# Two attention layers: score tiles in two PSUM pairs, one bank per accumulator, and other split steps in the second layer

## The chip, the cores and the metric

The kernel runs on one core of a Trainium2 chip. The metric is device time in microseconds (us), lower is better. Three runs of the kernel before took 3214.86, 3215.67 and 3217.78 us; their median is 3215.67. The engines are called PE (matmul), PEld (the weight loads ahead of matmuls, which overlap them), DVE (vector), ACT (scalar, activations), POOL and SP (which here mostly issue DMAs).

## The reference

The input x is (4, 64, 64, 256): four images of 4096 tokens with 256 channels, in float32. Two self-attention layers follow each other.

```
# layer 0, per image; x is 4096 x 256
q, k = x @ Wq + bq, x @ Wk + bk          # 4096 x 32
v = x @ Wv + bv                          # 4096 x 256
x = gamma * (softmax(q @ k.T) @ v) + x
# layer 1
f, g = x @ Wf + bf, x @ Wg + bg          # 4096 x 32 (keys, queries)
v = x @ Wh + bh                          # 4096 x 128
out = x + (softmax(g @ f.T) @ v) @ Wo + bo
```

## The kernel before

Both layers are done as flash attention without a running maximum: scores are computed transposed (keys on partitions), their exponential is the unnormalised weight p, p is multiplied with the values into PSUM, and the division by the sum comes at the end of a block of queries.

**Two kinds of product.** An fp32 matmul takes two records on PE for each instruction. An fp32r matmul takes one[...]. So a step can be *split*: ACT computes the exponential twice (`high`, L537, with a slightly lowered exponent and rounded to fp32r, and `p`, L539, in fp32), and DVE makes `low = p - high` (L543) and `d = high - 4096 low` (L548). Three fp32r products with three forms of the values (h, l, d) then give the fp32 product: h and l go to one accumulator, d to another, and at the block's end they are combined as `(1 + EPS) * first + second`. A step that is not split is called whole: it has one exponential and one fp32 product, which goes straight into the second accumulator.

**Layer 0** has 16 blocks of 256 queries per image, with 8 steps of 512 keys each. All steps are split. A step has four score matmuls of 256 columns (L527) and 24 products of 258 columns (L567): 256 channels, one column for the sum of the weights and one of padding. There are two halves of 128 queries, each with its two accumulators, so four accumulators in all. The block's end (`end_first`, L600, L601) copies the first accumulator of a half on ACT and adds the second on DVE; divisions, the residual and the output follow as small units in the next block's steps.

**Layer 1** has 8 blocks of 512 queries per image, with 16 steps of 256 keys each. A step has two score matmuls of 512 columns, and products with two 128-key tiles (L585). The steps in `SPLIT1` (2, 6, 10, 14) are split, the other twelve are whole. The sum of the weights is added up on DVE over the steps (L560; L558 adds the first two). The block's end (`end_second`) has two ACT copies of halves of the first accumulator (L637), two DVE adds of the second (L638) and a DVE add of the sum's two halves (L640). Then four output units, in steps 1 to 4 of the next block, each multiply 128 queries with Wo and compute their sum of weights on PE (L647, L648), and divide and store them.

**The order of work.** The main loop (L719 on) runs over all steps of both layers and all images. In step n it issues `cut_both` of n (d), `cut_low` of n+1, the sum's add of n, the scores and the exponentials of n+2, units that are due in this step, and the products of n. In layer 1 the d products of a split step come after the products of the step behind it. The units project the next stretch of tokens: layer 1's queries, keys and values while layer 0 runs (the last two in the first block of layer 1), and the next image's layer 0 while layer 1 runs (none in the last image). A unit transposes tokens (L389), splits them (L402, L403), multiplies them (L419, L461) and brings queries and keys through DRAM to their places (SP stores, POOL loads, L490). This is the order in which the kernel is written; the framework's scheduler may still move instructions of an engine past each other when it builds the program, and it adds the waits. Each engine runs its instructions in the built order.

**PSUM** has eight banks of 512 fp32 values per partition. `ps_st` holds one score tile of two banks, for both layers: the scores of step n+2 can be written when the exponentials of step n+1 have read it. `ps_acc` has four banks in rotation: layer 0 takes all four for a block, layer 1 takes two, so that one block's accumulators lie beside the next one's. `ps_side` has two banks for units. In SBUF the buffers that matter are tags "p" (three, whole p), "t" (two, `high`, and p of layer 1's split steps), "l" (two) and "d" (one: d of layer 0, the running sum of layer 1).

Of the kernel before, what the change touches and what calls it, by code (L numbers as in the profile page):

```python
# [49 lines left out]
F32 = mybir.dt.float32  # L50
F32R = mybir.dt.float32r
I32 = mybir.dt.int32
AF = mybir.ActivationFunctionType
# [3 lines left out]
P = 128  # L57
QB = 512
QB0 = 256
# [3 lines left out]
EPS = 2.0**-12  # L63
UP = 2.0**12
AHEAD = 3

SPLIT1 = (2, 6, 10, 14)

# [166 lines left out]
def fast_path(ctx: ExitStack, tc: tile.TileContext, x, w0, w1, wo, bo, gamma, out, off):  # L237

    nc = tc.nc
# [5 lines left out]
    W = C + 2  # L245
    assert C == 2 * P and CV == (C, P) and D == 32 and N % QB == 0
    G = (4, 2)
    NQ = (N // QB0, N // QB)
    NI = (N // (G[0] * P), N // (G[1] * P))
    NS = QB0 // P  # L250
# [5 lines left out]
    data = ctx.enter_context(tc.tile_pool(name="data", bufs=1))  # L256
    work = ctx.enter_context(tc.tile_pool(name="work", bufs=2))
    dram = ctx.enter_context(tc.tile_pool(name="dram", bufs=1, space=bass.MemoryType.DRAM))
    ps_st = ctx.enter_context(tc.tile_pool(name="ps_st", bufs=1, space=bass.MemoryType.PSUM))
    ps_acc = ctx.enter_context(tc.tile_pool(name="ps_acc", bufs=4, space=bass.MemoryType.PSUM))  # L260
    ps_side = ctx.enter_context(tc.tile_pool(name="ps_side", bufs=2, space=bass.MemoryType.PSUM))


# [106 lines left out]

    xT, x_parts, k_t, v_t, halves = {}, {}, {}, {}, {}
    qk_dram, x1_dram = {}, {}
    q_t, first_p, waiting = {}, [], {}


    def transpose_unit(b, l, h):
# [134 lines left out]
    class Step:  # L511
# [8 lines left out]
        def scores(self):  # L520
            b, l, j, i = self.b, self.l, self.j, self.i
            n = 2 * QB // G[l]
            q0 = j * n % QB
            st = ps_st.tile([P, G[l], n], F32, tag="st", name=f"st_{self.key}")
            for g in range(G[l]):
                kt = G[l] * i + g
                nc.tensor.matmul(  # L527
                    st[:, g, :],
                    k_t[b, l, kt // NT][:, kt % NT * P : (kt % NT + 1) * P],
                    q_t[b, l, j * n // QB][:, q0 : q0 + n],  # L530
                    start=True,
                    stop=True,
                )
            s_flat = st.rearrange("p g n -> p (g n)")
            if self.split:
                self.high = wide("t", f"high_{self.key}", F32R)
                nc.scalar.activation(self.high, s_flat, AF.Exp, bias=down)  # L537
            self.p = wide("t" if self.split and l == 1 else "p", f"p_{self.key}")
            nc.scalar.activation(self.p, s_flat, AF.Exp)  # L539
# [12 lines left out]
        def add_up(self, p_sum):  # L552
            if self.l == 0:
                return
            if self.i == 0:
                first_p.append(self.p)
            elif self.i == 1:
                nc.vector.tensor_add(p_sum, first_p.pop(0), self.p)  # L558
            else:
                nc.vector.tensor_add(p_sum, p_sum, self.p)  # L560

# [13 lines left out]
        def products_second(self, acc, parts):  # L575
            v = v_t[self.b, self.i]
            for part in parts:
                p, v_part, which, first, last = {
                    "h": lambda: (self.high, v["h"], 0, self.i == SPLIT1[0], False),
                    "l": lambda: (self.low, v["l"], 0, False, self.i == SPLIT1[-1]),  # L580
                    "d": lambda: (self.d, v["d"], 1, False, False),
                    "whole": lambda: (self.p, v, 1, self.first, self.last),
                }[part]()
                for g in range(G[1]):
                    nc.tensor.matmul(  # L585
                        acc[which],
                        v_part[:, g, :],
                        p[:, g * QB : (g + 1) * QB],
                        start=first and g == 0,
                        stop=last and g == G[1] - 1,  # L590
                    )
# [36 lines left out]

        return [residual(0), residual(1)]

    def end_second(b, j, acc, p_sum):
        key = f"{b}_{j}"
        o = []
        for h in range(QB // QB0):
            part = slice(h * QB0, (h + 1) * QB0)
            o.append(work.tile([P, W], F32, tag="o", name=f"o_{key}_{h}"))
            nc.scalar.activation(o[h][:, :QB0], acc[0][:, part], AF.Copy, scale=1.0 + EPS)  # L637
            nc.vector.tensor_add(o[h][:, :QB0], o[h][:, :QB0], acc[1][:, part])  # L638
        sums = work.tile([P, QB], F32, tag="sums", bufs=1, name=f"sums_{key}")
        nc.vector.tensor_add(sums, p_sum[:, :QB], p_sum[:, QB:])  # L640

        def output(t):
            def issue():
                tok = slice(t * P, (t + 1) * P)
                ps = side_psum(f"pso_{key}_{t}")
                part = o[t // NS][:, t % NS * P : (t % NS + 1) * P]
                nc.tensor.matmul(ps[:, :C], part, wo_sb, start=True, stop=True)  # L647
                nc.tensor.matmul(ps[:, C : C + 1], sums[:, tok], ones[:, :1], start=True, stop=True)  # L648
                n = (b * N + j * QB) // P + t
                nc.vector.reciprocal(inverse[:, 1, n : n + 1], ps[:, C : C + 1])  # L650

                y = small(f"y_{key}_{t}")
                nc.scalar.activation(y, ps[:, :C], AF.Copy, scale=inverse[:, 1, n : n + 1])  # L653
                row = j * QB + t * P
                nc.gpsimd.dma_start(out[b, row : row + P, :], y, accum_op=ALU.add)  # L655

            return issue

        return [output(t) for t in range(NT)]
# [15 lines left out]
    steps[1].scores()  # L675
    steps[0].cut_low()
    beyond = Step(B, 1, 0, 0)
    beyond.scores = nothing
    keys = [(b, l, j) for b in range(B) for l in range(2) for j in range(NB)][NB:]
    acc, p_sum, units = None, None, {}  # L680

# [33 lines left out]
    for n, s in enumerate(steps):  # L715
        b, l, j = s.b, s.l, s.j
        if s.first:
            units = plan(b, l, j, ends)
            acc = [  # L719
                ps_acc.tile([P, QB], F32, tag="acc", name=f"acc_{b}_{l}_{j}_{a}") for a in range(2 * NS if l == 0 else 2)  # L720
            ]
            if l == 1:
                p_sum = wide("d", f"p_sum_{b}_{j}")
        if l == 0 and s.last:
            x_res[b, j] = []
            for t in range(NS):
                x_res[b, j].append(small(f"x_res_{b}_{j}_{t}"))
                row = (j * NS + t) * P
                nc.sync.dma_start(x_res[b, j][t], x[b, row : row + P, :])
                nc.gpsimd.tensor_add(x_res[b, j][t], x_res[b, j][t], bv)  # L730

        ahead = steps[n + 3] if n + 3 < len(steps) else None
        if ahead is not None and ahead.first:
            k = (ahead.b, ahead.l, ahead.j * (QB0, QB)[ahead.l] // QB)
            if k not in q_t:
                load_q(*k)
        if b == l == j == 0 and s.i == 5:
            load_q(0, 0, 0, slice(QB0, QB), qk_dram[0, 0, 0].bitcast(F32R)[:, :, :, QB0:])
        after, later = (steps[n + k] if n + k < len(steps) else beyond for k in (1, 2))

        early = []
        if b == l == j == 0 and s.i + AHEAD < NB:
            early = [project_units(0, 0, 2 * (s.i + AHEAD) + k) for k in range(2)]
            run([u[0] for u in early])

        s.cut_both()
        after.cut_low()
        s.add_up(p_sum)
        todo = units.get(s.i, [])

        if l == 1:
            later.scores()
            run(todo)

            behind = steps[n - 1] if not s.first and steps[n - 1].split else None
            if s.last and behind:
                behind.products_second(acc, ("d",))
            s.products_second(acc, ("h", "l") if s.split else ("whole",))
            if not s.last and behind:
                behind.products_second(acc, ("d",))  # L760
        else:
            for half, what in ((0, "h"), (0, "l"), (1, "h")) if s.last else ((0, "h"), (1, "h")):
                s.products_first(acc, half, what)
            for half in () if s.last else (0, 1):
                s.products_first(acc, half, "l")
            if early:
                run(early[0][1:] + early[1][1:])
            later.scores()
            run(todo)
            for half, what in ((0, "d"), (1, "l"), (1, "d")) if s.last else ((0, "d"), (1, "d")):  # L770
                s.products_first(acc, half, what)

        over = (min(s.i + 2, NI[l] - 1) + 1) * G[l] // NT if j == NQ[l] - 1 else 0
        while keys and halves.get(keys[0]) == 2 and (keys[0][:2] == (b, l) or keys[0][2] < over):
            load_k(*keys.pop(0))
        if s.last:
            ends = end_first(b, j, acc) if l == 0 else end_second(b, j, acc, p_sum)
    run(ends)


# [67 lines left out]
```

## Time and profile before

| what | value |
|---|---|
| median of three runs | 3215.67 us |
| the profiled execution, and its span | 3218.27 us, 3216.5 us |
| granted PE clock | 0.997 |
| layer 0 stages, images 2 to 4 (elapsed) | 454.2, 453.5, 452.7 us |
| layer 1 stages, images 1 to 4 (elapsed) | 336.2, 336.3, 336.0, 312.6 us |
| DVE busy in the layer 1 stage of image 2 | 287.5 us |
| exponential p, 128x1024 (L539) | 1020 ns each |
| exponential high, 128x1024 (L537) | 1116 ns each |
| DVE add of the sum, 128x1024 (L560) | 1222 ns each |

The times are of one profiled execution. "Busy" is the time in which an engine had an instruction under way. A matmul's end is modelled, and matmuls overlap in the pipeline, so the mean duration of one is longer than the distance between two. "Idle before" is the time that an engine stood still ahead of an instruction, and the name after the arrow is what ended it. "Issue" there means that nothing visible was waited for.

### The profile page before, as it was taken

What the parts mean: (1) busy time and instruction counts of PE and PEld (TensorE: products, weight loads), DVE (VectorE), ACT (ScalarE), POOL (GpSimd) and SP (SyncE); (2) the same over time, 40 slices, a digit from 0 to 9 for tenths busy, and PEclk for the clock granted to TensorE, in tenths of its full rate; (3) what the DMA queues carried; (4) which work ended last, traced back from release to release, by engine and by line L of the source; (5) the groups of instructions that cost most, each with busy time, mean ns of one, the idle gap of its engine ahead of it and who ended that gap; (6) DMA issues with size and microseconds to landing.
All of it is one profiled execution on the core that took longest, in us unless ns stands there. A gap on an engine that the chain in (4) does not pass through costs nothing. (4 is left out here: it accounts for less than half of the span.)

```text
span 3216.5 us, 53556 instructions
## 1 busy us (share of the span) xinstructions
PE 3166.9 (98%) x19780; PEld 2637.3 (82%) x19780; DVE 2688.0 (84%) x3221; ACT 2081.7 (65%) x2771; POOL 758.6 (24%) x948
## 2 busy tenths in 40 slices
PE   8999999999999999999999999999999999999997
PEld 7999997666799999766679999966668999995554
DVE  7888888888888888888888888888888888887776
ACT  6666666666666666666666666666666666666564
POOL 5222223111322222211132222311123222241110
PEclk9999999999999999999999999999999999999999
DMA  4121113222311112322231121222222112131111
GB/s 117 43 50 49 46 49 73 38 40 42 60 45 50 49 44 54 67 40 41 41 63 41 47 52 46 66 52 40 44 48 51 46 46 52 43 74 27 24 22 16
DMA packets 368348, 155.56 MB, mean 48 GB/s; under 512 B 264112, under 2 KB 352688, under 8 KB 368080
## 3 DMA queue, kind: packets, MB, share of 16 engines
q1 hardware_dynamic: 322048, 100.76, 12.9%
q0 software_dynamic: 45120, 50.97, 9.5%
q8 instruction: 160, 2.62, 0.4%
q14 instruction: 108, 0.88, 0.1%
q10 hardware_dynamic: 912, 0.33, 0.0%
HBM read 82.58 MB, written 67.11 MB: 47 GB/s over the span
## 5 line engine op out<-in xcount | busy, mean ns | idle before, releaser
L539 ACT ACTIVATE p<-st 128x1024 f32<-128x1024 f32 x1024 | 1044.7, 1020 | 283.9 <-PE st L527 276.7
L537 ACT ACTIVATE high<-st,down 128x1024 fp32r<-128x1024 f32 x640 | 714.3, 1116 | 710.1 <-PE st L527 572.5
L543 DVE TENSOR_TENSOR low<-p,high 128x1024 fp32r<-128x1024 f32 x640 | 859.6, 1343 | 159.2 <-ACT p L539 159.2
L548 DVE SCALAR_TENSOR_TENSOR d<-low,high 128x1024 fp32r<-128x1024 f32 x640 | 788.6, 1232 | 227.7 <-PE acc L567 225.0
L527 PE MATMUL st<-q,k 128*128 128x256 f32 (+1 forms) x3072 | 744.8, 350 | 6.7 <-ACT p L539 5.4
L585 PE MATMUL acc<-p,v 128*128 128x512 f32 x1536 | 735.6, 596 | 0.0
L527 PEld LDWEIGHTS st<-q,k 128*128 128x128 f32 x3072 | 455.9, 189 | 192.2 <-ACT p L539 130.7
L567 PE MATMUL acc<-v0d,d 128*128 128x258 f32 x4096 | 593.1, 284 | 2.6 <-DVE d L548 2.2
L567 PE MATMUL acc<-v0h,high 128*128 128x258 f32 x4096 | 588.5, 283 | 1.2 <-ACT high L537 1.2
L567 PE MATMUL acc<-v0l,low 128*128 128x258 f32 x4096 | 588.3, 283 | 0.6 <-DVE low L543 0.5
L560 DVE TENSOR_TENSOR p_sum<-p_sum,p 128x1024 f32<-128x1024 f32 x448 | 547.3, 1222 | 14.2 <-ACT p L539 3.6
L567 PEld LDWEIGHTS acc<-v0h,high 128*128 128x128 f32 x4096 | 534.5, 190 | 1.6 <-ACT high L537 1.4
L567 PEld LDWEIGHTS acc<-v0d,d 128*128 128x128 f32 x4096 | 530.5, 189 | 5.2 <-DVE d L548 4.5
L567 PEld LDWEIGHTS acc<-v0l,low 128*128 128x128 f32 x4096 | 532.3, 189 | 1.1 <-DVE low L543 1.0
L585 PEld LDWEIGHTS acc<-p,v 128*128 128x128 f32 x1536 | 282.5, 189 | 186.5 <-issue 158.8
L624 POOL TENSOR_TENSOR x_res<-x,bo 128x256 f32<-128x256 f32 x128 | 200.8, 1569 | 891.2 <-DVE x L613 891.1
L490 POOL DMA_DIRECT2D q<-qk_dram x256 | 127.4, 509 | 706.0 <-PE st L527 701.4
L655 POOL DMA_DIRECT2D out<-y x128 | 113.0, 891 | 507.6 <-ACT y L653 502.3
L461 PE MATMUL psv<-wv,xT 128*128 128x128 f32 (+1 forms) x1024 | 196.6, 332 | 2.7 <-DVE v0d L479 1.4
L730 POOL TENSOR_TENSOR x_res<-x_res,bv 128x256 f32<-128x256 f32 x128 | 171.0, 1336 | 72.7 <-DMA x_res<-in_x 72.5
L461 PEld LDWEIGHTS psv<-wv,xT 128*128 128x128 f32 x1024 | 160.0, 193 | 20.4 <-DVE v0d L479 2.2
L490 POOL DMA_DIRECT2D k<-qk_dram x224 | 113.4, 524 | 221.0 <-PE st L527 109.2
(97 smaller groups left out, 2069.5 us busy)
## 6 DMA issues: line engine op xcount, KB each, us to landing
x_res<-in_x SPq DMA_DIRECT2D x128, 128.0 KB, 2.1
qk_dram<-qk_parts SPq DMA_DIRECT2D x128, 128.0 KB, 1.8
x_dram<-x SPq DMA_DIRECT2D x128, 128.0 KB, 1.7
out<-x_res SPq DMA_DIRECT2D x128, 128.0 KB, 1.7
squares<-x_dram SPq DMA_DIRECT2D x512, 32.0 KB, 2.0
out<-y POOLq DMA_DIRECT2D x128, 128.0 KB, 3.1
q<-qk_dram POOLq DMA_DIRECT2D x252, 64.0 KB, 2.2
k<-qk_dram POOLq DMA_DIRECT2D x224, 64.0 KB, 2.1
```

Source lines behind the costliest of these rows:

```text
L461: nc.tensor.matmul(ps[:, t, :], xT[key][:, c, t * P : (t + 1) * P], wv[l][:, c, :], start=(c == 0), stop=(c == NCC - 1),)
L490: nc.gpsimd.dma_start(dst[n * D : (n + 1) * D, :], parts[h, which])
L527: nc.tensor.matmul(st[:, g, :], k_t[b, l, kt // NT][:, kt % NT * P : (kt % NT + 1) * P], q_t[b, l, j * n // QB][:, q0 : q0 + n], start=Tru ...
L537: nc.scalar.activation(self.high, s_flat, AF.Exp, bias=down)
L539: nc.scalar.activation(self.p, s_flat, AF.Exp)
L543: nc.vector.tensor_sub(self.low, self.p, self.high.bitcast(F32))
L548: nc.vector.scalar_tensor_tensor(self.d, self.low.bitcast(F32), -UP, self.high.bitcast(F32), ALU.mult, ALU.add)
L560: nc.vector.tensor_add(p_sum, p_sum, self.p)
L567: nc.tensor.matmul(acc[2 * s + which][:, :W], p[:, g * QB0 + s * P : g * QB0 + (s + 1) * P], v0[self.i][v][:, g, :], start=self.first and ...
L585: nc.tensor.matmul(acc[which], v_part[:, g, :], p[:, g * QB : (g + 1) * QB], start=first and g == 0, stop=last and g == G[1] - 1,)
L624: nc.gpsimd.tensor_add(x_old[s], x_new[s], bo_sb)
L730: nc.gpsimd.tensor_add(x_res[b, j][t], x_res[b, j][t], bv)
```

## The change

The score tiles and accumulators of both layers move into one pool, `ps_main`, with named places: "st" (two banks), "pair" (two banks), "acc0" and "acc1" (one bank each). In layer 1 the scores of a step go to "pair" if the step's number within the image is even and not 0, and to "st" otherwise, so two score tiles alternate. Its two accumulators are acc0 and acc1 in every block. In layer 0 the scores stay in "st", and the third and fourth accumulators are the two halves of one "pair" tile.

The split steps become 0, 4, 8 and 12. So the first step of a block is split and writes the first accumulator alone, and the last is whole and writes the second one alone; the second one's first product is now that of step 1. The running sum starts as a copy of p of step 0, and every later step adds. The ACT copies of the first accumulator become a function of their own, `take_first_two`, which is called in the last step ahead of the scores of n+2. In layer 0, the first step of a block takes the order of products that only the last had: first half h and l, second half h, and then, after the scores and units, d, l, d.

```diff
-SPLIT1 = (2, 6, 10, 14)
+SPLIT1 = (0, 4, 8, 12)
...
-    ps_st = ctx.enter_context(tc.tile_pool(name="ps_st", bufs=1, space=bass.MemoryType.PSUM))
-    ps_acc = ctx.enter_context(tc.tile_pool(name="ps_acc", bufs=4, space=bass.MemoryType.PSUM))
+    ps_main = ctx.enter_context(tc.tile_pool(name="ps_main", bufs=1, space=bass.MemoryType.PSUM))
     ps_side = ctx.enter_context(tc.tile_pool(name="ps_side", bufs=2, space=bass.MemoryType.PSUM))
...
-            st = ps_st.tile([P, G[l], n], F32, tag="st", name=f"st_{self.key}")
+            index = j * NI[1] + i
+            tag = "pair" if l == 1 and index > 0 and index % 2 == 0 else "st"
+            st = ps_main.tile([P, G[l], n], F32, tag=tag, name=f"st_{self.key}")
...
             if self.i == 0:
-                first_p.append(self.p)
-            elif self.i == 1:
-                nc.vector.tensor_add(p_sum, first_p.pop(0), self.p)
+                nc.vector.tensor_copy(p_sum, self.p)
             else:
                 nc.vector.tensor_add(p_sum, p_sum, self.p)
...
-                    "whole": lambda: (self.p, v, 1, self.first, self.last),
+                    "whole": lambda: (self.p, v, 1, self.i == 1, self.last),
...
-    def end_second(b, j, acc, p_sum):
-        key = f"{b}_{j}"
+    def take_first_two(b, j, acc):
+
         o = []
         for h in range(QB // QB0):
-            part = slice(h * QB0, (h + 1) * QB0)
-            o.append(work.tile([P, W], F32, tag="o", name=f"o_{key}_{h}"))
-            nc.scalar.activation(o[h][:, :QB0], acc[0][:, part], AF.Copy, scale=1.0 + EPS)
-            nc.vector.tensor_add(o[h][:, :QB0], o[h][:, :QB0], acc[1][:, part])
+            o.append(work.tile([P, W], F32, tag="o", name=f"o_{b}_{j}_{h}"))
+            nc.scalar.activation(o[h][:, :QB0], acc[0][:, h * QB0 : (h + 1) * QB0], AF.Copy, scale=1.0 + EPS)
+        return o
+
+    def end_second(b, j, acc, p_sum, o):
+        key = f"{b}_{j}"
+        for h in range(QB // QB0):
+            nc.vector.tensor_add(o[h][:, :QB0], o[h][:, :QB0], acc[1][:, h * QB0 : (h + 1) * QB0])
...
-            acc = [
-                ps_acc.tile([P, QB], F32, tag="acc", name=f"acc_{b}_{l}_{j}_{a}") for a in range(2 * NS if l == 0 else 2)
-            ]
+            acc = [ps_main.tile([P, QB], F32, tag=f"acc{a}", name=f"acc{a}_{b}_{l}_{j}") for a in range(2)]
+            if l == 0:
+                pair = ps_main.tile([P, 2, QB], F32, tag="pair", name=f"acc_pair_{b}_{j}")
+                acc += [pair[:, a, :] for a in range(2)]
...
         if l == 1:
+            if s.last:
+                o = take_first_two(b, j, acc)
             later.scores()
             run(todo)
...
-            for half, what in ((0, "h"), (0, "l"), (1, "h")) if s.last else ((0, "h"), (1, "h")):
+
+            edge = s.first or s.last
+            for half, what in ((0, "h"), (0, "l"), (1, "h")) if edge else ((0, "h"), (1, "h")):
                 s.products_first(acc, half, what)
-            for half in () if s.last else (0, 1):
+            for half in () if edge else (0, 1):
                 s.products_first(acc, half, "l")
...
-            for half, what in ((0, "d"), (1, "l"), (1, "d")) if s.last else ((0, "d"), (1, "d")):
+            for half, what in ((0, "d"), (1, "l"), (1, "d")) if edge else ((0, "d"), (1, "d")):
                 s.products_first(acc, half, what)
```

More of the change, by code (lines that the diff above doesn't have):

```diff
@@ L372, in fast_path @@
     qk_dram, x1_dram = {}, {}
-    q_t, first_p, waiting = {}, [], {}
+    q_t, waiting = {}, {}
     def transpose_unit(b, l, h):
@@ L677, in fast_path @@
     beyond = Step(B, 1, 0, 0)
-    beyond.scores = nothing
+    beyond.scores, beyond.split = nothing, False
     keys = [(b, l, j) for b in range(B) for l in range(2) for j in range(NB)][NB:]
@@ L776, in fast_path @@
         if s.last:
-            ends = end_first(b, j, acc) if l == 0 else end_second(b, j, acc, p_sum)
+            ends = end_first(b, j, acc) if l == 0 else end_second(b, j, acc, p_sum, o)
     run(ends)
```

## The prediction

> **What bounds the kernel now.** The page's busy times come first. The clock is at full speed (0.997), and PE is busy almost throughout:
>
> ```profile
> PE 3166.9 (98%) x19780; PEld 2637.3 (82%) x19780; DVE 2688.0 (84%) x3221; ACT 2081.7 (65%) x2771; POOL 758.6 (24%) x948
> ```
>
> A busy PE with modelled ends can hide bubbles, so I asked for the stages (elapsed, then busy PE, PEld, DVE, ACT, POOL): a first-layer stage, then a second-layer stage, both of the second image.
>
> ```profile
> 858.90:1313.10 454.20, 452.98 (x3769) 451.93 (x3768) 384.09 (x450) 298.27 (x377) 121.44 (x126) 1.00 0.21 50
> ...
> 1313.10:1649.40 336.30, 333.50 (x1163) 204.63 (x1162) 287.54 (x344) 219.12 (x311) 60.65 (x98) 1.00 0.27 47
> ```
>
> In the first layer the weight loads fill 451.93 of 454.20 us: nothing to win. In the second PE is still the engine with most to do, but its load row has room, and the view of the waits says what the loads wait for (total, times, longest):
>
> ```profile
> PEld acc L585 <- issue: 219.7, 917, 0.2
> PEld st L527 <- ACT p L539: 130.7, 357, 1.6
> ...
> PEld acc L585 <- DVE d L548: 11.7, 16, 1.3
> ...
> PEld pso L647 <- DVE o L638: 3.8, 10, 1.4
> ```
>
> The first row is no stall: an fp32 product's loads stand 0.43 us apart and take 0.19, so 219.7/917 = 0.24 us of gap is normal. Take that off the second row: 130.7 - 357 x 0.24 = 45 us of real stall of score matmuls behind the exponential. A second count agrees. The usual start-to-start distances in the trace are 429 ns for an fp32 record (a product is two), 233 for a 512-column fp32r one, 120 for 258 columns, 216/112 for the projection and output records. Counted over the four second-layer stages they make 325+325+325+291 us, against 336+336+336+313 elapsed; without the last block's drain the excess is 45 us. In the first layer it is 1.6 to 3 us per image after the first.
>
> The timeline shows one such stall (start, duration, engine, what):
>
> ```profile
> 2952.57 0.72 PE L527 MATMUL st<-q,k 128*128 128x512 f32 x2
> ...
> 2953.39 1.11 ACT L537 ACTIVATE high<-st,down 128x1024 fp32r<-128x1024 f32 x1 [0.87 <-PE st L527]
> ...
> 2954.40 1.02 ACT L539 ACTIVATE p<-st 128x1024 f32<-128x1024 f32 x1
> ...
> 2955.45 1.22 DVE L543 TENSOR_TENSOR low<-p,high 128x1024 fp32r<-128x1024 f32 x1 [1.67 <-ACT p L539]
> 2955.47 0.44 PEld L527 LDWEIGHTS st<-q,k 128*128 128x128 f32 x2 [0.42 <-ACT p L539]
> ```
>
> A split step's scores hold the only score tile through two activations, 1.11 + 1.02 us. PE has one whole step, 4 x 0.43 = 1.72 us, to put in between, then waits. By step, most of the 45 us lies right after split steps (3, 7, 11, 15: 28 us) and at steps 1 and 13 (12 us).
>
> **What the Trainium skill says.** "Perfetto Trace Analysis", Optimization Strategy: the same gap repeating on the engine that should be saturated can mean too little PSUM for the next tile. It does here. Same page, Identifying the Most-Contended Engine: matmul busy time is a bad measure, loads are better. It agrees: 98% busy hides the 45 us. "PSUM — Partial Sum Buffer", Terms: eight banks of 2 KiB, so a 128x1024 fp32 score tile is two; the plan is full before (2 + 4 + 2) and after (2 + 2 + 1 + 1 + 2).
>
> **The change, part by part.**
>
> *Second pair for scores.* Scores of step n+2 now wait for the exponential of n, which PE needs next anyway, not of n+1. Nearly all 45 us go. The pair is free for it because the accumulators shrink from four rotating banks to two: -45.
>
> *One bank per accumulator.* Step 0 is split, so a new block starts on acc0, whose copies (L637, 0.39 us each) move ahead of the last exponential: their input, the low product of step 12, is long done. They sit on ACT (65% busy, two steps of slack): 0. acc1 gets its first product, step 1's fp32 one, only when both DVE adds of the old block (L638, 0.41 each) are done; and an output matmul that needs the first add now stands just before it. By the built order, PE issues after the old block's last product: scores 0.47, high and low 0.93, scores 0.47, output matmul. That is 1.87 us from its last issue. DVE meanwhile has low (1.22), copy (0.69, below), d (1.22), add, add, in that order at most boundaries. The scores of step 0 stand 2.66 us before that last product begins; the two activations end about 0.25 us after it begins, so low, copy and d end near 3.4 us and the first add near 3.85, where PE arrives at 1.72 + 1.87 = 3.6. A wait of 0.3 us, at 16 of 28 boundaries (in six the adds stand before d), and 0.4 at the six where projection work is in front: +7. Behind it on PE stand all later products, on DVE the next sum. acc1 itself is free by then.
>
> *Copy.* The split first step needs a copy into the sum before the next add: 32 more DVE instructions. None of this shape is in the trace. Lower bound 0: DVE idles 336.3 - 287.5 = 49 us per second-layer stage. For its length, "VectorE: DVE Perf Modes", The perf-mode tier table, gives an fp32 SBUF copy double rate (1227 ns at 2048); halved by its fixed-term formula, (512+151)/0.96 = 691 ns, an estimate; the trace's 128x512 add takes 680, which fits. Upper bound: single rate like the adds, 1.22 us. I take 0.69: 5.5 us per stage, hidden in the 49. But in the unit-laden middle of the stage DVE was busy for 223 of 260 us (1350 to 1610); with six copies, and 6 us fewer to do it in, that is 228 of 254, 90%, and low or d will at times be late: +4, bounds 0 and +15.
>
> *Split steps 0, 4, 8, 12.* Same count, same records: 0. But the block's first two steps now bring low, d and copy together with the old block's sums and adds; that is in the +7.
>
> *First block of each image.* The key half of the last projection goes psqk, ACT, DVE, DRAM and POOL loads; before, it landed about 11.3 us after psqk, with 13.7 us of PE work between. In the built order the projection stands later and 9.9 us of work remain ahead of step 14's scores: 1.4 us each, four times: +6. POOL's and SP's queues are otherwise as before but for neighbours that swap.
>
> *First layer.* acc2 and acc3 become one tile, so its first write waits for DVE's last add of the old block as well; and the first step is ordered like the last, which brings the need for d forward by 0.7 us. The timeline of an old boundary prices it:
>
> ```profile
> 380.91 1.12 PE L567 MATMUL acc<-v0h,high 128*128 128x258 f32 x8
> 381.15 1.22 DVE L548 SCALAR_TENSOR_TENSOR d<-low,high 128x1024 fp32r<-128x1024 f32 x1
> 381.62 0.39 ACT L600 ACTIVATE o<-acc 128x258 f32<-128x258 f32 x1
> ...
> 382.29 0.42 DVE L601 TENSOR_TENSOR o<-o,acc 128x258 f32<-128x258 f32 x1
> ```
>
> New order from 380.91: acc0 high and low 0.96, scores 0.47, two filler products 0.24, then d at 382.58 (ready 382.37), then the pair at 383.06 (ready 382.71). It fits. In 12 of 60 boundaries d ends 0.2 us or so too late: +3.
>
> Sum: -45 + 7 + 4 + 6 + 3 = -25 us. The profiled execution took 3218.27 (span 3216.5 and 1.8 around it), so 3193; the median stands 2.6 lower, at 3215.67: **3191 us**.
>
> **Rivals.**
> *All of it:* DVE and the key chain keep up; 3216 - 45 = 3171. For it: DVE and ACT have room on average. Against: the two queues are in order.
> *DVE takes the place of the wait:* boundary waits of 0.8 us rather than 0.3 (+16 over 32 blocks) because DVE begins a 1.2 us operation just ahead of the adds: 3207, and to 3219 where low and d come late too. For it: DVE is 84% busy and gets work, packed at the boundary. Against: it idles 34 us per stage before low, waiting for ACT.
> *Slower, first layer:* the merged pair's wait. If the old block's last add ends later than the 2.15 us after the new block's first product at which the pair is wanted, all 60 boundaries stall. It ends at 1.79 in most, 2.18 at worst. It decides when it costs over (25 + 6.4)/60 = 0.52 us each, an add near 2.7 us; at 0.7 us each, 3191 + 42 = 3233.
> *That nothing changes:* excluded as "no effect": the built order has the alternate tiles.
>
> **How the numbers follow.** Forecast (3178 to 3206 on its own) 0.62, all of it 0.10, DVE 0.20, slower 0.08. Faster or slower by 0.2%, about what a measurement of this kernel can tell from no change, is 6.4 us, so 3209 and 3222. About half of DVE's case lies in between: faster 0.81, same 0.11, slower 0.08. The range 3174 to 3212 leaves out about half of "all of it", a third of DVE's case and the slow one.
>
> **What would show it.** Right: loads of scores waiting for p fall from 130.7 us to under 60, and each of the first three second-layer stages from 336 to about 330 us, the last (313) to about 305; first-layer stages within 2 us of 454; small new waits of the output matmul's load on DVE's add. Wrong: acc or pso loads waiting over 20 us in all for DVE's adds, low or d; pair products waiting for the first layer's add; a copy of 1.2 us; scores waiting for key loads for more than 2 us per image.

## The result, and the profile after

The changed kernel takes 3175.35 us (median of four runs, 3173.95 to 3176.02), where the kernel before takes 3216.73 us beside it (3214.86 to 3218.65). The ratio is 0.9871, with a 95% interval of 0.9854 to 0.9888. Its profiled execution took 3175.03 us, with a span of 3173.3 us. The forecast was 3191 us: the sign and the place were right, the gain came out 16 us larger.

The page of the changed kernel, its busy times:

```profile
PE 3135.8 (99%) x19780; PEld 2652.2 (84%) x19780; DVE 2708.7 (85%) x3253; ACT 2086.0 (66%) x2771; POOL 772.8 (24%) x948
```

PE has the same 19780 records and DVE its 32 copies more. The two stages of the second image again, first layer and then second layer (elapsed, then busy PE, PEld, DVE, ACT, POOL):

```profile
848.70:1302.00 453.30, 453.21 (x3767) 452.05 (x3766) 385.80 (x450) 298.09 (x377) 125.41 (x126) 1.00 0.21 51
1302.00:1628.50 326.50, 325.40 (x1164) 208.16 (x1163) 290.64 (x352) 220.42 (x313) 61.10 (x98) 1.00 0.27 48
```

The first layer is where it was (454.2 before). The second fell from 336.3 to 326.5 us, though DVE does 3 us more in it. By image the second layer's stages went 336.2, 336.3, 336.0, 312.6 to 326.5, 326.6, 326.9, 298.6: together 1321.1 to 1278.7, or -42.4 us. The first layer's four are 1.1 us longer in sum, and the time up to the kernel's first product was 2.3 us shorter (28.0 to 25.7 us). That last part does not look like the change's: in the experiments below, with and without it, this time lies between 24.9 and 27.1 us.

What the loads wait for after the change (total, times, longest):

```profile
PEld acc L586 <- issue: 229.4, 957, 0.2
...
PEld st L530 <- ACT p L542: 18.2, 69, 1.1
...
PEld psqk L420 <- ACT xh L403: 7.4, 10, 1.5
...
PEld pso L652 <- DVE o L643: 4.1, 16, 1.3
```

Score loads waiting for p fell from 130.7 us (357 times) to 18.2 (69 times); with 0.24 us of normal gap taken off each, from 45 us to 1.6. The second layer's products no longer wait for d beyond the normal gap: that row was 11.7 us and is now 1.0 us in 4 gaps of 0.24. One row grew: projections waiting for the rounded tokens `xh`, from 1.6 us (3 times) to 7.4 (10 times); the last experiment shows what it is.

The boundary that the forecast priced at 0.3 us, in the last image (start, duration, engine, what):

```profile
2969.27 2.14 ACT L542 ACTIVATE p<-st 128x1024 f32<-128x1024 f32 x2
...
2970.19 1.88 PE L586 MATMUL acc<-p,v 128*128 128x512 f32 x4
2970.32 1.23 DVE L546 TENSOR_TENSOR low<-p,high 128x1024 fp32r<-128x1024 f32 x1 [0.38 <-ACT p L542]
...
2971.47 0.69 DVE L559 COPY p_sum<-p 128x1024 f32<-128x1024 f32 x1
...
2972.07 1.22 DVE L551 SCALAR_TENSOR_TENSOR d<-low,high 128x1024 fp32r<-128x1024 f32 x1
...
2973.21 0.74 DVE L643 TENSOR_TENSOR o<-o,acc 128x256 f32<-128x256 f32 x2
...
2973.76 0.61 PE L652 MATMUL pso<-wo,o 128*128 128x256 f32 x2
```

DVE does what was foretold, in the order foretold: low, copy, d, two adds. The first of the two adds began at 2973.21; at 0.41 us for one it ended at 2973.62. The output matmul starts on PE at 2973.76, right after the scores before it (the record ahead of it starts 0.23 us earlier, the usual distance). There is no hole on PE.

### The profile page after: what moved, and what is told of

The parts are those of the page before. It is cut to its first block, busy times and chain, and to the rows that moved or that the text cites. A ratio compares the mean times of both kernels' runs of the same rounds, so it can differ in the third digit from the quotient of the medians.

```text
span 3173.3 us, 53569 instructions
## 1 busy us (share of the span) xinstructions
PE 3135.8 (99%) x19780; PEld 2652.2 (84%) x19780; DVE 2708.7 (85%) x3253; ACT 2086.0 (66%) x2771; POOL 772.8 (24%) x948
## 3 DMA queue, kind: packets, MB, share of 16 engines
q1 hardware_dynamic: 322048, 100.76, 13.1%
## 4 chain that ended last, share of the span: by engine, by line
PE 94%; issue 3%; DVE 1%; ACT 1%; DMA 1%; POOL 0%; SPq 0%; DVEq 0%; ACTq 0%; POOLq 0%
PE acc L586 24%; PE acc L568 23%; PE acc_pair L568 23%; PE st L530 15%; PE psv L462 5%; PE psqk L420 2%; PE pso L652 2%; PE pso L653 0%; DVE d L551 0%; DVE p_sum L561 0%; POOL out L660 0%; DMA k<-qk_parts 0%; DVE low L546 0%; ACT p L542 0%; DMA wv<-in_L_conv_Wv 0%
## 5 line engine op out<-in xcount | busy, mean ns | idle before, releaser
L568 PE MATMUL acc<-v0d,d 128*128 128x258 f32 x2048 | 338.5, 286 | 1.0 <-DVE d L551 0.5
L568 PE MATMUL acc<-v0l,low 128*128 128x258 f32 x2048 | 330.5, 283 | 0.6 <-DVE low L546 0.5
L568 PE MATMUL acc_pair<-v0l,low 128*128 128x258 f32 x2048 | 330.7, 282 | 0.0
L568 PE MATMUL acc_pair<-v0h,high 128*128 128x258 f32 x2048 | 329.5, 283 | 0.0
L568 PE MATMUL acc_pair<-v0d,d 128*128 128x258 f32 x2048 | 329.2, 283 | 0.0
L568 PEld LDWEIGHTS acc<-v0h,high 128*128 128x128 f32 x2048 | 287.5, 190 | 3.1 <-issue 1.4
L568 PEld LDWEIGHTS acc<-v0d,d 128*128 128x128 f32 x2048 | 280.4, 189 | 3.8 <-DVE d L551 3.1
L568 PEld LDWEIGHTS acc<-v0l,low 128*128 128x128 f32 x2048 | 281.8, 190 | 1.3 <-DVE low L546 1.2
L568 PEld LDWEIGHTS acc_pair<-v0h,high 128*128 128x128 f32 x2048 | 282.6, 189 | 0.0
L568 PEld LDWEIGHTS acc_pair<-v0l,low 128*128 128x128 f32 x2048 | 281.6, 189 | 0.0
```

What stands on the lines that cost most here:

```text
L568: nc.tensor.matmul(acc[2 * s + which][:, :W], p[:, g * QB0 + s * P : g * QB0 + (s + 1) * P], v0[self.i][v][:, g, :], start=self.first and ...
```

## The experiments

The second layer's time in those that change it most, as the sum of its four stages. The column "plain block" is a block of the last image without projections, from its first product to the next block's: the third to the seventh block there, which agree within 0.03 us.

| kernel | split steps | score tiles | accumulators | second layer, us | plain block, us | median, us |
|---|---|---|---|---|---|---|
| before | 2, 6, 10, 14 | 1 | four rotating | 1321.1 | 37.53 | 3216.73 |
| e7_only_split_steps | 0, 4, 8, 12 | 1 | four rotating | 1308.0 | 36.80 | 3201.95 |
| e1_one_score_tile | 0, 4, 8, 12 | 1 | one bank each | 1313.0 | 37.27 | 3210.53 |
| e2_old_split_steps | 2, 6, 10, 14 | 2 | one bank each | 1295.7 | 36.42 | 3195.83 |
| after | 0, 4, 8, 12 | 2 | one bank each | 1278.7 | 36.21 | 3175.35 |

**Without the second score tile.**

```diff
-            tag = "pair" if l == 1 and index > 0 and index % 2 == 0 else "st"
+            tag = "st"
```

> From the changed kernel, with the second score tile alone undone: all scores of layer 1 go to "st"; split steps, accumulators and layer 0 stay as changed. Theory (the second score tile brings the gain, and the waits of products on DVE's low and d were a consequence of the late exponentials): 3209 to 3222 us, that is 34 to 46 above the changed kernel; score loads waiting for p back above 110 us in all; loads of acc waiting for d or low back at over 6 us. Rival (the new split steps and the accumulators bring it): 3175 to 3188 us, and score loads that wait for p little longer than the 20 us of the changed kernel.

Measured: 3210.53 us (3208.27 to 3212.4), 0.9975 of the kernel before (0.9966 to 0.9984). That is 35 us above the changed kernel, and 34.3 us of it are in the second layer by the table. So with the new split steps in place the second tile carries most of the gain. Its waits:

```profile
PEld st L530 <- ACT p L542: 130.3, 338, 1.6
...
PEld pso L652 <- DVE o L643: 8.1, 13, 1.3
```

The first row is back at its old size. But the loads of acc that waited for d did not come back, so the part of the theory that called them a consequence of late exponentials falls. The second row is new, and it is the boundary wait of the forecast. In the last image:

```profile
3039.71 0.75 DVE L643 TENSOR_TENSOR o<-o,acc 128x256 f32<-128x256 f32 x2
3040.18 0.30 PEld L652 LDWEIGHTS pso<-wo,o 128*128 128x128 f32 x2 [0.59 <-DVE o L643]
```

With 0.24 us normal, 0.59 is a stall of 0.35 us, close to the forecast's 0.3. With these split steps it is there only with one score tile. PE then has the last record of the old block and 1.4 us of high, low and one pair of scores ahead of the output matmul. With two tiles a second pair of scores (0.47 us) stands there as well, and covers it.

**The split position alone.** From the kernel before; also the copy that starts the sum.

```diff
-SPLIT1 = (2, 6, 10, 14)
+SPLIT1 = (0, 4, 8, 12)
...
             if self.i == 0:
-                first_p.append(self.p)
-            elif self.i == 1:
-                nc.vector.tensor_add(p_sum, first_p.pop(0), self.p)
+                nc.vector.tensor_copy(p_sum, self.p)
...
-                    "whole": lambda: (self.p, v, 1, self.first, self.last),
+                    "whole": lambda: (self.p, v, 1, self.i == 1, self.last),
...
-    beyond.scores = nothing
+    beyond.scores, beyond.split = nothing, False
```

> From the kernel before, with split steps 0, 4, 8, 12 and the copy as first sum, and nothing else: one score tile, four rotating accumulators. Theory (second score tile): between 3209 and 3226 us, no gain of over 6 us; score loads wait over 110 us for p. Rival (split position): 3176 to 3195 us. If the products' waits on DVE's low and d (about 10 us before) go away by the new position alone, 3203 to 3209 us and score loads still waiting.

Measured: 3201.95 us (3200.13 to 3204.32), 0.9949 (0.9933 to 0.9966). Neither main theory had it. The second layer is 13.1 us shorter although its score loads wait as much as before:

```profile
PEld st L527 <- ACT p L539: 134.3, 336, 1.6
...
PEld acc L583 <- DVE low L543: 3.9, 3, 1.3
```

What went is the wait for d, from 11.7 us in 16 gaps to 1.0 in 4 gaps of 0.24: with the normal gap taken off, 7.9 us. The kernel before shows it near the end of a block in its last image:

```profile
3003.81 1.22 DVE L548 SCALAR_TENSOR_TENSOR d<-low,high 128x1024 fp32r<-128x1024 f32 x1
...
3004.11 0.62 PE L585 MATMUL acc<-low,v 128*128 128x512 f32 x2
...
3005.08 0.30 PEld L585 LDWEIGHTS acc<-d,v 128*128 128x128 f32 x2 [0.79 <-DVE d L548]
...
3005.89 0.19 PEld L585 LDWEIGHTS acc<-p,v 128*128 128x128 f32 x1
```

The order of the products goes with it. The d products of steps 2, 6 and 10 stand behind the whole product of the step after them, four records of 0.43 us between low and d in all 32 blocks, and none of their loads waits for d. In a block's last step the loop turns this round: the d products of step 14 go ahead of the whole product of step 15 (the load at 3005.89), in all 32 blocks. All 16 gaps in the row are of step 14; here it is 0.79 - 0.24 = 0.55 us. With split steps 0, 4, 8 and 12 no split step stands just ahead of the last one, and the trace has the four records in front of every d. The plain block is 0.73 us shorter, and these 0.55 us are most of it. The rest of the 13.1 us was not taken apart. Nor did a run keep the old split steps and change only the order of these two products, so the part that the order alone would bring is argued from the traces.

**Two score tiles, but the old split position.**

```diff
-SPLIT1 = (0, 4, 8, 12)
+SPLIT1 = (2, 6, 10, 14)
...
-                    "whole": lambda: (self.p, v, 1, self.i == 1, self.last),
+                    "whole": lambda: (self.p, v, 1, self.first, self.last),
```

> From the changed kernel, with the split steps back at 2, 6, 10, 14 and the second accumulator begun in step 0: two score tiles and one bank per accumulator stay. The first product of a block then goes to the bank that both DVE adds of the old block have to leave first. Theory (split steps at 0 are what makes one bank per accumulator free of cost): 28 boundaries at 0.7 to 1.5 us, so 3195 to 3217 us, the loads of acc waiting for DVE's o by 20 us or more. Rival (the adds are early enough in either order, or the loads run ahead): 3171 to 3181 us.

Measured: 3195.83 us (3194.49 to 3197.38), 0.9932 (0.9915 to 0.9948), 20 us above the changed kernel. The size is at the lower edge of the theory, but not by its mechanism: no load of acc waits for o. The waits are

```profile
PEld acc L586 <- DVE d L551: 13.5, 23, 1.3
...
PEld pso L652 <- DVE o L643: 7.8, 13, 1.4
...
PEld acc L586 <- ACT high L540: 5.8, 7, 1.2
```

Less 0.24 us each these are 8.0, 4.7 and 4.1 us, together 16.8. The split position costs 17.0 us in the second layer here (1295.7 against 1278.7). It is the late d again (all 23 gaps are of step 14), and in blocks with units the wait for `high`. What I had thought, that it protects the merged accumulators, is a small part: the loads of the output matmul, which in the plain blocks stands ahead of the new block's first product, wait 4.7 us for DVE's adds, against 0.3 in the changed kernel (4.1 - 16 x 0.24).

**Layer 0's first step in its old order.**

```diff
-            edge = s.first or s.last
+            edge = s.last
```

> From the changed kernel, with layer 0's first step in the order that it had before (both halves' high products first); the merged pair stays. The pair is then wanted 0.48 us after the block's first product, where the old block's last add ends 1.79 us after it. Theory (the reordering is what hides the merged tile's wait): about 1.3 us at each of 60 boundaries, 3230 to 3260 us, all of it in the four layer 0 stages. Rival (a wait shorter than that is swallowed because the weight loads run ahead): 3173 to 3190 us.

Measured: 3174.35 us (3173.63 to 3174.78), 0.9865 (0.9849 to 0.9882): no loss at all. The theory took the written order for the built one. In the traces only 78 of the 19780 records on PE differ, place by place, from the changed kernel's. At this kernel's boundaries PE runs

```profile
905.43 0.64 PE L568 MATMUL acc<-v0h,high 128*128 128x258 f32 x4
...
907.20 0.42 DVE L602 TENSOR_TENSOR o<-o,acc_pair 128x258 f32<-128x258 f32 x1
...
907.80 0.64 PE L568 MATMUL acc_pair<-v0h,high 128*128 128x258 f32 x4
```

The merged pair is first written 2.37 us after the block's first product (905.43 to 907.80), 0.18 us after the old block's last add ends (907.62). The framework's scheduler gave it that place under either written order: the 78 records lie at few of the 60 boundaries.

**That new order alone, from the kernel before.**

```diff
-            for half, what in ((0, "h"), (0, "l"), (1, "h")) if s.last else ((0, "h"), (1, "h")):
+            for half, what in ((0, "h"), (0, "l"), (1, "h")) if s.first or s.last else ((0, "h"), (1, "h")):
```

(and the same condition in the two loops behind it)

> From the kernel before, with the new order of products in layer 0's first step alone. Theory (it neither costs nor brings time by itself; it only pays for the merged pair): 3213 to 3220 us. Rival (d is wanted 0.7 us earlier and comes late at some boundaries, as forecast at 0.2 us in 12 of 60 or more): 3219 to 3230 us. Rival (it is a gain of its own): under 3210 us.

Measured: 3219.94 us (3215.3 to 3222.7) against 3218.45, ratio 1.0001 (0.9992 to 1.001). No effect of it shows. The interval leaves room for 0.1% (3 us) either way, so the time alone does not exclude the forecast's 2.4 us (0.2 us at 12 boundaries); but the first layer's loads that wait for d are no more than before, 3.9 us in 8 gaps against 4.5 in 9.

**A longer copy.**

```diff
-                nc.vector.tensor_copy(p_sum, self.p)
+                nc.vector.tensor_tensor(p_sum, self.p, self.p, ALU.max)
```

> From the changed kernel, with the copy that starts a block's sum made 0.53 us longer (a maximum of p with itself, 1.22 us like the adds, in place of the 0.69 us copy), 32 times. Theory (DVE has slack at the boundary, and the weight loads take up the waits of the output matmul): 3172 to 3180 us. Rival (the output matmul's wait on DVE's first add is already on the path, as the forecast's +7 us had it): 0.3 to 0.5 us at 22 to 28 boundaries, 3182 to 3190 us.

Measured: 3176.92 us (3176.43 to 3181.12), 0.9875 (0.9858 to 0.9891). In its trace 17 us more of DVE (32 times 0.53) lengthen the second layer by 1.9 us, nearly all in the sixth block of images 1 to 3, about 0.5 us each. DVE thus has slack at most boundaries, as the theory says. The rival is right at three: where the sixth block of images 1 to 3 begins, the load of the output matmul waits 0.73 us for the add, 0.49 more than normal, and that is the 0.5 us. At the other boundaries inside an image it does not wait; there, in the places looked at, the built order answers the longer operation by putting the two adds ahead of d. So the run does not price the boundary in its old order.

**The last projection earlier.**

```diff
-                put(6 * n, t), put(6 * n + 2, qk), put(6 * n + 3, v)
+                put(4 * n, t), put(4 * n + 2, qk), put(4 * n + 3, v)
```

> From the changed kernel, with the last projection of layer 1's keys begun two steps earlier in the first block of each image (steps 4, 6, 7 in place of 6, 8, 9). Theory (the stall of 1.2 to 1.8 us ahead of step 14's scores is the key's way through DRAM): it goes, in three or four images, 3168 to 3172 us. Rival (the stall is of something else, or crowding the units costs what it brings): 3173 to 3179 us.

Measured: 3175.37 us (3173.7 to 3177.02). The built order is that of the changed kernel, record for record on PE, DVE, ACT and POOL; the scheduler seems to have placed the projection by its inputs already. So the run decided nothing about the stall. It shows how well a median repeats: 3175.35 and 3175.37.

**The last tile of tokens read back earlier.**

```diff
+            if l == 1 and h == NH - 2:
+                load_squares((b, 1, h + 1), waiting.pop((b, h + 1)))
             whole = data.tile([2 * D, QB0], F32, tag="qk", name=f"qk_{b}_{l}_{h}")
...
             elif l == 1:
-                load_squares((b, 1, h + 1), waiting.pop((b, h + 1)))
+                if h != NH - 2:
+                    load_squares((b, 1, h + 1), waiting.pop((b, h + 1)))
```

> From the changed kernel: in the first block of layer 1, SP issues the eight loads that read the last tile of tokens back (L278) ahead of the key store of the tile before it (L444), where six of them stood behind that store for over 2 us; in the built order the last projection's first product stands one product group earlier on PE. Theory (the stall of 1.8 us ahead of step 14's scores is the end of the chain tokens, projection, keys through DRAM): it shrinks by 0.5 to 1.8 us in images 1 to 3, 3170 to 3174 us. Rival (the chain is held by the order on ACT, DVE and PE, not by the loads): 3174.5 to 3178 us, stall as it was.

Measured: 3173.23 us (3172.7 to 3173.98), 0.986 (0.9843 to 0.9876). In the changed kernel SP's queue reads, in the first image,

```profile
531.35 0.81 SPq L278 DMA_DIRECT2D squares<-x_dram  x2
533.72 0.34 SPq L444 DMA_DIRECT2D qk_dram<-qk_parts  x1
534.11 2.91 SPq L278 DMA_DIRECT2D squares<-x_dram  x6
```

and in this one

```profile
530.94 3.92 SPq L278 DMA_DIRECT2D squares<-x_dram  x8
534.96 0.39 SPq L446 DMA_DIRECT2D qk_dram<-qk_parts  x1
```

The median falls into the theory's window, and the stages of images 1 to 3 are 0.7, 0.7 and 1.0 us shorter. But it is not by the key chain. What PE waits for ahead of step 14's scores in the changed kernel is a record in front of them, the first projection of the *next* image's first tile:

```profile
552.16 1.22 DVE L561 TENSOR_TENSOR p_sum<-p_sum,p 128x1024 f32<-128x1024 f32 x1
...
553.30 0.70 DVE L390 STREAM_TRANSPOSE xT<-squares 128x512 f32<-128x512 f32 x1
554.03 0.62 ACT L403 CAST xh<-xT 128x512 fp32r<-128x512 f32 x1 [1.92 <-DVE xT L390]
...
554.71 0.38 PE L420 MATMUL psqk<-xh,wqk 128*128 128x256 f32 x1 [1.11 <-ACT xh L403]
```

Its tokens were there (the last of their loads landed at 550.95), but on DVE their transpose stood behind d of step 12 and an add of the sum. In this run the transpose comes before that add:

```profile
551.93 0.70 DVE L390 STREAM_TRANSPOSE xT<-squares 128x512 f32<-128x512 f32 x1
...
552.56 1.18 DVE L564 TENSOR_TENSOR p_sum<-p_sum,p 128x1024 f32<-128x1024 f32 x1
552.67 0.62 ACT L403 CAST xh<-xT 128x512 fp32r<-128x512 f32 x1 [0.79 <-DVE xT L390]
...
553.34 0.39 PE L420 MATMUL psqk<-xh,wqk 128*128 128x256 f32 x1
```

From the start of the last d record to that of this projection it takes 0.37 us in place of 1.50, where 0.23 is usual; some of that comes back in the second block, which is 0.35 us longer. The keys do not come sooner: counted from the start of the stage, the last of them lands after 30.4 to 30.8 us in the changed kernel and after 30.4 to 31.0 here. In the first image that is at 552.74, and PE is free for step 14's scores only at 553.43. The last image settles it: its keys take the same way, no next image is projected, and nothing waits there in either kernel.

So the key chain is not this stall. It belongs to the split position: PE waits for the next image's `xh` at this place, 1.1 to 1.2 us in each of images 1 to 3, in the three kernels of the table with split steps 0, 4, 8, 12, and not in the two with 2, 6, 10, 14. The transpose is a unit of step 12, which is now a split step. This is the fastest kernel of the study, but its 2.1 us on the changed kernel (0.07%) are less than medians tell from no change; it is the trace's stages that show them.

## Why the prediction was right, and where it was short

**The bound and the direction.** The stall of score matmuls behind a split step's two exponentials was real, it was what a second score tile removes, and DVE, ACT and PSUM's reshaping allowed it. The one-tile run gives it back: 34.3 us of second-layer time.

**The term of -45 had about the right size and one cause too few.** It named the second score tile alone. But the table shows that the second tile alone does not do it: with the old split position it leaves 17.0 us of this layer standing, and the split position brings 13.1 us without a second tile. My step said "Split steps 0, 4, 8, 12. Same count, same records: 0". That is the step that failed. The count of records is the same; the place of the d products is not, and the row that told of it (acc waiting for d, 11.7 us in 16 gaps) stood in the fence that I showed. I had two counts of 45 us that agreed, one of score loads and one of PE's excess, and took their agreement for proof that nothing else was in it. It was not proof: with the split position alone the first count comes to 54 us (134.3 - 336 x 0.24), more than before, and the layer is 13.1 us shorter. A load that waits is not PE time lost as long as earlier records are still running. So it was in part luck that -45 fitted.

**The boundary term (+7) measured nothing.** The order and the operations were right. The first add was put 3.85 us after the last product begins and ended after 3.43 (2970.19 to 2973.62), and PE's arrival, put at 3.6, was 3.57. Of the 0.42 us between, 0.06 is my sum, whose own terms give 3.79, and 0.15 is the exponential: it ended 0.10 us after that product begins, and I had 0.25. The rest is mainly that I added durations. Low, copy, d and the first add started 1.15, 0.60 and 1.14 us apart, where the recorded durations that I summed are 1.22, 0.69 and 1.22: 0.24 us less. A wait of 0.3 us is gone with that. The 0.35 us in the run with one score tile shows that such a wait exists, and that it hangs on one pair of scores.

**The DVE load term (+4) measured nothing where it was put.** In the changed kernel no second-layer product waits longer than the normal gap for low, d or high. DVE was busy for 290.64 of 326.50 us, and 17 us more of it cost 1.9. Where DVE did come late was the projection ahead of step 14's scores. The copy itself took 0.69 us. That agrees with the estimate of 691 ns, for which I had the double rate of an fp32 copy from the Trainium skill, "VectorE: DVE Perf Modes", The perf-mode tier table.

**The key chain (+6) had the size by luck and the wrong cause.** From the first record of the projection the keys landed after 10.1 us (542.65 to 552.74 in the first image), where I had 11.3, and PE had 10.8 us of work in between (to 553.43), where I had 9.9. They were in time. What stands at this place is the wait for the next image's `xh`, 1.27 us over the usual distance in images 1 to 3. In the last image it is another wait: the scores of steps 14 and 15 stand one behind the other, and the scores after them wait 0.86 us for p. Together that is 4.7 us.

**The first layer (+3) came to +1.1**, within what its stages differ between runs. Its loads wait no more for d than before: 3.1 us in 10 gaps, against 4.5 in 9.

Added up for the second layer: forecast -45 + 7 + 4 + 6 = -28, measured -42.4. With +7 and +4 at nothing and the +6 at 4.7, some -47 us are left for what the forecast gave -45. This is bookkeeping, and no run measured that figure by itself. The measured 3175 us is 3 us below the likeliest case's own range of 3178 to 3206, and by only 1.4 us inside the range of 3174 to 3212. Of the rivals, "all of it" at 3171 came nearest: DVE kept up with the products, and the keys were in time. DVE's taking the place of the wait is excluded by the waits after, and the merged pair's stall by the order in which the pair is written.

## What to carry to other kernels

Before you credit one edit with a stall, look at every row of waits in the stage that the other edits could move too, and ask what stands in front of each waiting product: a product whose input comes late wants other work between it and the one before. When a wait shrinks after an edit, read which record waits and for what, before you take the edit's theory as shown. Where a wait of a few tenths decides, add the distances between starts that the timeline shows and not the recorded durations, and read the built order: two edits of the written order here changed next to nothing of it. Edits interact: here one bank per accumulator, with the copies moved ahead, cost 5.0 us with one score tile (1308.0 to 1313.0), and with two and the same split steps no hole was left at that boundary.

## What the hardware showed

Two things I had not expected. Operations in a row on DVE and on ACT start 0.07 to 0.10 us before the recorded end of the one before (an exponential of 1.11 us, and the next starts 1.01 us after it; low of 1.23 us, and the copy 1.15 after it), so a chain on one engine is shorter than its sum of durations. And a weight load's wait is no hole on PE by itself: at the changed kernel's boundaries a load of the output matmul waits 0.18 us for DVE, and the matmul still follows the one before it at the usual distance.
